# One stationary operand of 96 columns in the last tile's transform back over y

## The chip, the cores and the metric

The kernel runs on 1 core of one Trainium2 chip. The metric is the device time of one execution in microseconds (us), as the median of several runs; beside it stands one profiled execution, from which all views of the trace come.

## The reference, cut to what matters

The input x has 64 samples of 96 channels of 56 by 56 pixels. Layer 0 normalizes it, computes for each of the 6144 (sample, channel) images a 7 by 7 filter of its own by a small network, convolves every image with its filter (zero padding 3), and adds the result to x. Layer 1 treats the result as tokens of 96 channels: a Fourier mixer over the 3136 tokens of a sample, then a feed-forward network in 8-bit floats.

```
weight = a.reshape(b * c, 1, KS, KS)
out = jax.lax.conv_general_dilated(xin, weight, window_strides=(1, 1),
    padding=[(pad, pad), (pad, pad)], feature_group_count=b * c, ...)
x = x + _L0_conv_ref(_gn(x), ...)
t = _to_tokens(x)
t = t + _L1_attn_ref(_ln_t(t), ...)
t = t + _L1_ffn_ref(_ln_t(t), ...)
```

## The kernel before, in words

The program has two phases, one after the other: `conv_layer` (line 699) writes x1 to device memory, and `fourier_layer` (line 1313) reads it. They use the same on-chip memory in turn, so the second phase's pools open when the first one's close.

*Convolution phase.* The 6144 images are cut into tiles of at most 126 (`ROWS`, line 149): 48 tiles of 126 and a last one, tile 48, of 96. The convolution is done as a product in the frequency domain: transforms of the image over y and x as small matmuls, a product with the filter's spectrum, and transforms back over x and over y. Between the steps over x and over y the data goes through device memory (`turn_x`, `turn_y`) to bring another index onto the partitions.

*The transform back over y.* An image's 56 columns are handled in 7 chunks of 8, and the chunks in groups (0,1), (2,3), (4,5), (6). For each chunk `load_x` (line 1104) loads V from `turn_y`: 128 partitions (two halves of 64) by 4 sets of the tile's images. There are 3 buffers for V. `back_y` (line 1108) then takes, for each of the 4 sets and each half, V's images as the stationary operand (64 rows by the images as columns) and the constant `inv_y` as the moving one (64 rows by 56 columns). The result has the images on partitions, in two PSUM banks for a group, one for each half. The images are cut into pieces of 64: a tile of 126 has operands of 64 and 62 columns, the last tile of 64 and 32. After a group, `keep_even` (line 1140, ScalarE) copies the even half to a buffer e (there is one), and `apart` (line 1130, VectorE) makes sum and difference into a buffer o (there are two); `store` (line 1151) writes o to x1, two transfers for a chunk. In the profile these tiles are called V, s (the PSUM banks), e, o and x.

*Order of the work.* Each phase puts its steps, with a cost and a due time each, into a `Plan` (line 292); `emit` (line 344) plays them against a model of the engines and calls them in the order that comes out. All engine calls go through a helper that pins this order on each engine, which is why the profile gives line 505 for every instruction. The step of `back_y` has the planned cost 0.48 us for each chunk (line 1241), whatever the tile. All loads and stores of the phase are issued by SyncE (SP), in order; a transfer that has to wait for a buffer holds up what is queued behind it.

*Around the end of the phase.* Tile 48 is the last one through every step, so its `back_y` is the last work of the phase on TensorE. The Fourier phase then loads its constants (`dft`, `inv`) from ScalarE's queue and its first tokens (`t` from `x`) from SP's queue.

Of the kernel before, what the change touches and what calls it, by code (L numbers as in the profile page):

```python
# [698 lines left out]
def conv_layer(tc, nc, x, x1, b0, attn_bias, weights, a, f, con):  # L699
# [6 lines left out]
    with ExitStack() as ctx:  # L706
# [8 lines left out]
        def bank(name, tag="ps"):  # L715
            return psp.tile([128, BANK], F32, tag=tag, bufs=BUFS1[tag], name=name)
# [117 lines left out]
        def images(i):  # L834
            return min(ROWS, n_rows - i * ROWS)

        def tile_(i, T, at, e0):

            r0 = i * ROWS
            n = images(i)  # L840
# [267 lines left out]
            def back_y(cs):  # L1108


                for half in range(2):
                    v["s4", cs[0], half] = bank(f"s4_{i}_{cs[0]}_{half}")
                for at_, c in enumerate(cs):
                    for e in range(4):
                        other = 6 - e if e < 3 else 7
                        lo = CHUNK // 2 * at_
                        for half in range(2):
                            for a in range(0, n, 64):
                                z = min(a + 64, n)
                                both = v["s4", cs[0], half][a:z, lo : lo + CHUNK // 2].rearrange(  # L1120
                                    "p (x y) -> p x y", x=8
                                )
                                rows_ = slice(64 * half, 64 * half + 64)
                                nc.tensor.matmul(
                                    both[:, e : other + 1 : other - e],
                                    v["V", c][rows_, e * ROWS + a : e * ROWS + z], inv_y[rows_],
                                    start=True, stop=True,
                                )
# [82 lines left out]
            def convolve(T):  # L1211
# [21 lines left out]
                for cs in ((0, 1), (2, 3), (4, 5), (6,)):  # L1233
                    c0, k = cs[0], len(cs)
                    R = T + 2 * PERIOD1 + 14 + e0 * PERIOD1 + K * cs[-1]
                    s4 = [nm("ps", "s4", c0, half) for half in range(2)]
                    o, even = nm("o", c0), nm("e", c0)
                    for c in cs:
                        add(R - 6 - K * (cs[-1] - c) - 31.9, "SP", 0.5, lambda c=c: load_x(c),
                            r=[("dy", i, q) for q in range(4)], w=[nm("V", c)], lag=3.0)  # L1240
                    pe(R + 19.3, 0.48 * k, lambda cs=cs: back_y(cs), r=[nm("V", c) for c in cs],
                       w=[*s4, even, o], kind="halves")
                    add(R - 36.3, "ACT", 0.2 + 0.22 * k, lambda cs=cs: keep_even(cs), r=[s4[0], sm],
                        w=[even])
                    add(R + 103.7, "DVE", 0.12 + 0.54 * k, lambda cs=cs: apart(cs), r=[s4[1], even],
                        w=[o])
                    for c in cs:
                        add(R + 11.8 + c - c0, "SP", 0.8, lambda c=c: store(c), r=[o], lag=3.0)
# [764 lines left out]
```

## Time and profile before

| | us |
|---|---|
| median of 3 runs | 6463.43 (6441.33 to 6465.24) |
| profiled execution, its own time | 6475.86 |
| span in the profile | 6474.1 |
| TensorE matmul (PE) busy | 6132.8 (95%) |
| TensorE weight load (PEld) busy | 4108.4 |
| VectorE (DVE) busy | 4812.8 |
| ScalarE (ACT) busy | 4352.8 |
| GpSimd (POOL) busy | 1891.7 |
| mean granted TensorE clock | 0.975 of full speed |

How to read it: busy times are of one profiled execution. Matmuls overlap in the array, so a group's busy time and the mean duration of one instruction don't tell at what rate they follow each other; for that one looks at start times. A kernel's fp32 matmul appears as two passes, each with a weight load, in the records. In 40 equal slices of the span, PE is busy nine tenths or more in all but four slices: the first, the last, and two from 2266 to 2590 us where the convolution phase ends, with 8 and 7 tenths; the granted clock is down to 5 tenths in the second of these.

```profile
PE   8999999999999987999999999999999999999997
...
PEclk9999999999999995999999999999999999999998
```

### The profile page before, as it was taken

The page shows a single profiled execution, that of the slowest core. Times are in us where ns is not written, and L with a number is a line of the kernel's source. Part 1 is how long each engine was busy: PE and PEld are TensorE (multiplying, and loading weights), DVE is VectorE, ACT ScalarE, POOL GpSimd, SP SyncE. Part 2 cuts the span into 40 slices and gives each one's busy share as a digit, 9 for nine tenths or more (in the row PEclk, how much of TensorE's full clock was granted, in tenths as well). Part 3 has the DMA queues.
Part 4 walks back from the last instruction along what each step waited for, and adds up shares of the span by engine and source line. Part 5 has one row for each costly group of instructions (what it writes and reads, how often), then busy time and mean ns, then how long its engine had stood idle before and what let it go on. Part 6 is the DMA issues. An engine that isn't in the chain of part 4 may idle for free.

```text
span 6474.1 us, 219839 instructions
## 1 busy us (share of the span) xinstructions
PE 6132.8 (95%) x88899; PEld 4108.4 (63%) x88899; DVE 4812.8 (74%) x10984; ACT 4352.8 (67%) x10262; POOL 1891.7 (29%) x1816
## 2 busy tenths in 40 slices
PE   8999999999999987999999999999999999999997
PEld 3444444444444445877777777777777777777774
DVE  4555555555555642788888888988998899899988
ACT  3444444444444441788888888888888888888887
POOL 0222222122222220133333333333333333333334
PEclk9999999999999995999999999999999999999998
DMA  4677777777777876677777778777787787877775
GB/s 130 177 211 220 214 221 220 214 223 219 214 220 214 221 203 161 192 206 225 221 223 230 225 218 231 227 224 229 227 227 220 223 228 225 232 226 230 225 211 163
DMA packets 1325193, 1387.43 MB, mean 214 GB/s; under 512 B 738395, under 2 KB 1190558, under 8 KB 1317145
## 3 DMA queue, kind: packets, MB, share of 16 engines
q1 hardware_dynamic: 1322408, 1363.79, 74.5%
q8 instruction: 701, 11.49, 0.8%
q10 hardware_dynamic: 1769, 9.57, 0.5%
q14 instruction: 315, 2.58, 0.1%
HBM read 744.77 MB, written 628.13 MB: 212 GB/s over the span
## 4 chain that ended last, share of the span: by engine, by line
PE 28%; DMA 14%; ACT 9%; DVE 7%; issue 4%; SPq 1%; POOL 1%; POOLq 0%; ACTq 0%; DVEq 0%
PE l_psum L505 27%; DMA mv<-norms 3%; DMA Y<-turned 3%; ACT h L505 3%; DMA norms<-mr 2%; ACT t L505 2%; DMA nb<-copies 2%; DMA U<-turned 2%; SPq L505 1%; DVE h L505 1%; ACT y L505 1%; PE s L505 1%; DVE x L505 1%; DVE mv L505 1%; DVE g L505 1%
## 5 line engine op out<-in xcount | busy, mean ns | idle before, releaser
L505 PE MATMUL pm<-w0g,xT 128*126 128x512 f32 (+3 forms) x2450 | 1129.3, 602 | 3.0 <-ACT xT L505 3.0
L505 POOL TENSOR_TENSOR t<-t,t 128x504 f32<-128x504 f32 (+1 forms) x392 | 489.9, 1255 | 1954.2 <-DVE t L505 1953.9
L505 POOL TENSOR_TENSOR t<-t,y 96x448 f32<-96x448 f32 x448 | 607.4, 1356 | 1380.5 <-DVE y L505 1032.9
L505 PE MATMUL l_psum<-w1c,t 96*64 96x193 f32 (+1 forms) x7168 | 858.9, 348 | 37.9 <-DMA t<-x 16.7
L505 PEld LDWEIGHTS pm<-w0g,xT 128*126 128x126 f32 (+3 forms) x2450 | 434.0, 188 | 518.1 <-issue 511.3
L505 POOL TENSOR_TENSOR nb<-t,nb 96x448 f32<-96x448 f32 x448 | 532.9, 1194 | 708.1 <-DMA nb<-copies 610.9
L505 ACT COPY B<-s 120x504 f32<-120x504 f32 (+1 forms) x392 | 207.6, 580 | 775.3 <-PE s L505 719.3
L505 ACT COPY t<-l_psum 128x384 f32<-128x384 f32 (+1 forms) x1408 | 644.8, 493 | 57.1 <-PE l_psum L505 56.3
L505 ACT CAST h<-l_psum 128x448 f16<-128x448 f32 x1344 | 667.5, 566 | 14.6 <-PE l_psum L505 14.3
L505 DVE SCALAR_TENSOR_TENSOR g<-l_psum,st,nb 120x192 f32<-120x192 f32 x1792 | 646.3, 409 | 11.5
L505 PE MATMUL l_psum<-dft,Y 112*64 112x112 f32 (+1 forms) x11264 | 629.7, 263 | 4.5 <-DMA Y<-turned 1.8
L505 PEld LDWEIGHTS l_psum<-dft,Y 112*64 112x64 f32 (+1 forms) x11264 | 550.4, 138 | 125.5 <-issue 75.1
L505 DVE TENSOR_TENSOR t<-s,W 128x504 f32<-128x504 f32 (+1 forms) x784 | 481.3, 671 | 182.5 <-PE s L505 182.5
L505 PEld LDWEIGHTS l_psum<-w1c,sq 96*64 96x64 f32 (+1 forms) x7168 | 575.0, 138 | 46.5 <-ACT sq L505 1.9
L505 PE MATMUL l_psum<-inv,U 120*64 120x112 f32 (+1 forms) x7168 | 422.0, 265 | 61.3 <-DMA U<-turned 22.7
L505 PEld LDWEIGHTS l_psum<-inv,U 120*56 120x56 f32 (+1 forms) x7168 | 346.9, 134 | 171.3 <-ACT mr L505 39.9
L505 PEld LDWEIGHTS l_psum<-w1c,t 96*56 96x56 f32 (+1 forms) x7168 | 399.6, 138 | 85.0 <-issue 44.6
L505 PE MATMUL l_psum<-w1c,sq 96*64 96x1 f32 (+1 forms) x7168 | 451.5, 183 | 1.3 <-ACT sq L505 1.3
L505 PE MATMUL l_psum<-g,dft 56*64 56x192 f32 x7168 | 432.4, 340 | 14.3 <-DVE g L505 5.5
L505 DVE CAST h<-h 128x1344 fp8e5<-128x1344 f16 x448 | 413.9, 924 | 14.0 <-ACT h L505 10.4
L505 DVE COPY A<-s 128x504 f32<-128x504 f32 (+1 forms) x343 | 219.6, 674 | 267.2 <-PE s L505 240.3
L505 POOL TENSOR_SCALAR w<-w 128x448 f32<-128x448 f32 (+3 forms) x512 | 273.7, 536 | 464.5 <-DVE w L505 460.4
(127 smaller groups left out, 12513.3 us busy)
## 6 DMA issues: line engine op xcount, KB each, us to landing
turned<-t SPq DMA_DIRECT2D x640, 384.0 KB
nb<-copies SPq DMA_DIRECT2D x448, 336.0 KB
Y<-turned SPq DMA_DIRECT2D x192, 672.0 KB
Y<-turn_x SPq DMA_DIRECT2D x768, 110.2 KB
turn_y<-B SPq DMA_DIRECT2D x768, 110.2 KB
V<-turn_y SPq DMA_DIRECT2D x336, 252.0 KB
U<-turned SPq DMA_DIRECT2D x896, 90.0 KB
t<-x SPq DMA_DIRECT2D x448, 168.0 KB
```

What stands on the lines that cost most here:

```text
L505: ins = issue(*args, **kw)
```

## The change

In `back_y` the width into which a tile's images are cut becomes 64 only for tiles of more than 96 images; a smaller tile is taken in one piece. Only the last tile is smaller: its 96 images become one stationary operand of 96 columns instead of two of 64 and 32, and its 112 matmuls become 56. Nothing else is edited; the planned costs are the same.

```diff
             def back_y(cs):
 
 
+                width = 64 if n > 96 else n
                 for half in range(2):
                     v["s4", cs[0], half] = bank(f"s4_{i}_{cs[0]}_{half}")
                 for at_, c in enumerate(cs):
...
                         for half in range(2):
-                            for a in range(0, n, 64):
-                                z = min(a + 64, n)
+                            for a in range(0, n, width):
+                                z = min(a + width, n)
                                 both = v["s4", cs[0], half][a:z, lo : lo + CHUNK // 2].rearrange(
```

## The prediction

> **What bounds the kernel now.** I read the page first (PE busy 95% of the span), and then asked which stage the 56 removed matmuls stand in. All instructions carry one line number, so I went by tile names: the groups of the convolution phase, kept apart by shape, show what the change touches (count | busy us, mean ns of one | idle before).
>
> ```profile
> L505 PE MATMUL s<-inv_y,V 64*64 64x56 f32 x5488 | 256.8, 228 | 133.1 <-ACT B L505 67.4 <-DMA V<-turn_y 37.5 <-ACT W L505 25.9
> ...
> L505 PE MATMUL s<-inv_y,V 64*62 64x56 f32 x5376 | 226.7, 225 | 0.0
> ...
> L505 PE MATMUL s<-inv_y,V 64*32 64x56 f32 x112 | 21.9, 297 | 0.0
> ```
>
> Each fp32 matmul is two passes in the records. The 48 tiles of 126 images use 64 and 62 columns; only the last tile uses 64 and 32: 112 matmuls, 224 passes. By mean duration they look harmless (297 ns against 228), but matmuls overlap, so durations say little. The timeline of the PE does say it; tile 47 first (32 passes are one chunk):
>
> ```profile
> 2461.58 2.08 PE L505 MATMUL s<-inv_y,V 64*64 64x56 f32 x64 [4.26 <-DMA V<-turn_y]
> 2463.95 1.11 PE L505 MATMUL s<-inv_y,V 64*64 64x56 f32 x32 [0.29 <-DMA V<-turn_y]
> 2468.98 2.11 PE L505 MATMUL s<-inv_y,V 64*64 64x56 f32 x64 [3.92 <-DMA V<-turn_y]
> 2472.12 1.11 PE L505 MATMUL s<-inv_y,V 64*64 64x56 f32 x32 [1.03 <-DMA V<-turn_y]
> 2474.48 1.23 PE L505 MATMUL s<-inv_y,V 64*64 64x56 f32 x32 [1.25 <-DMA V<-turn_y]
> ```
>
> Then the chain that ended last, where tile 48 does the same amount of passes:
>
> ```profile
> 2474.00 2.97 DMA V<-turn_y
> 2477.11 38.92 PE s L505 x220
> ...
> 2516.11 0.45 ACT e L505
> ...
> 2517.88 5.13 DMA x<-o
> ...
> 2525.93 9.00 DMA t<-x
> ```
>
> 224 passes take 7.6 us of PE in tile 47 and 38.9 us in tile 48, and those 38.9 us are one unbroken piece of the chain. The windows (PE, PEld, DVE, ACT, POOL busy, then clock, DMA share, GB/s) show that nothing covers them, and that the clock is the same, half, in both tiles:
>
> ```profile
> 2461.50:2476.50 15.00, 7.64 (x224) 6.86 (x224) 3.81 (x8) 2.35 (x4) 0.00 (x0) 0.50 0.85 221
> 2477.10:2516.10 39.00, 38.99 (x222) 25.32 (x222) 3.44 (x6) 1.89 (x3) 0.00 (x0) 0.50 0.26 68
> 2516.10:2533.40 17.30, 0.63 (x4) 0.31 (x5) 0.73 (x4) 0.44 (x1) 0.83 (x8) 0.50 0.81 196
> 2533.40:2617.00 83.60, 75.72 (x830) 61.82 (x832) 31.85 (x99) 33.23 (x100) 2.24 (x4) 0.57 0.59 168
> 2617.00:6474.00 3857.00, 3710.79 (x66120) 2860.32 (x66115) 3385.76 (x8222) 3256.93 (x8414) 1398.14 (x1404) 0.99 0.77 221
> ```
>
> The Fourier layer starts only after this tail: its first load (t<-x) is issued once the last convolution store (x<-o) has landed, and it reuses the memory. So the tail is a serial seam of the program: whatever it loses, the span loses.
>
> **The change, part by part.**
>
> *Removed: 112 matmuls alternating between 64 and 32 columns.* In tile 48 one pair (64, then 32 columns) takes 38.92 / 56 = 0.695 us, so 0.35 us per matmul; in tile 47 a matmul takes 2.08 / 32 = 0.065 us. The surplus, 38.9 - 7.6 = 31.3 us, comes with the alternation of widths, because moving operand, clock and neighbours are the same. Here a rule of the skill speaks against the change: "TensorEngine Tiling (Array Packing)", Theoretical Speedup, says that operands of at most 64 by 64 let four tiles of the array work at once, so that one operand of 96 columns, which needs the whole width, leaves two. By that rule alone the old form would run in rounds of four passes as in tile 47 (56 rounds x 0.11 = 6.2 us), and the change would cost some 3 us. The row says 38.9. The same page (Key Properties) has the reason: changing the tiling mode, and not just the tile, drains the engine. 64 and 32 columns are two modes, 64 and 62 one. I take the row.
>
> *Added: 56 matmuls (112 passes) of 96 columns, all of one mode,* on two tiles of the array (rows 0-63 and 64-127), which write to different banks. No row shows this shape. From tile 47: (2.08 - 0.31 of the last pass) / 16 = 0.111 us for a round of four passes with 64 columns to load, 1.73 ns per column. From this:
> - if the round follows the weight load: 96 x 1.73 = 0.166 us, 56 rounds = 9.3 us;
> - if it follows the moving operand (56 columns as before): 0.111 us, 6.2 us;
> - if the two halves do not overlap: 112 x 0.166 = 18.6 us; if a drain remained at each matmul, 56 x 0.35 = 19.6 us.
>
> I take 9.3 us, 1.33 us per chunk instead of 5.56, as tile 47 shows that passes on different parts of the array overlap when the width stays. A negative cost beyond this is excluded: it would need less than no time for 112 passes.
>
> *Moved: nothing.* The order and the waits of ACT, DVE, POOL and SP are the same in the changed kernel, and those of PE outside these matmuls (the planner's costs are not edited). Tiles of 126 images keep width 64.
>
> *What is late next.* With PE fast, the tail becomes a loop of loads and stores in SP's queue. V has 3 buffers, so the load of chunk 3 waits for chunk 0, and SP issues in order: V3, V4, four stores of chunks 0 and 1, V5, V6, then stores. I replay it with durations of before (V load 2.97, e 0.63 and 0.44, o 1.15 and 0.68, four stores 1.74, two 0.78):
> - chunks 0, 1, 2: 2477.1 to 2481.2 (their V were issued at 2474.00 and 2476.03, before the tail; unchanged);
> - V3 issued at 2478.6 (before: 2482.84), lands 2481.6; chunk 3 to 2483.0, chunk 4 to 2484.4;
> - chunks 0 and 1 read out: e, o from 2480.0 to 2481.95, stores issued until 2483.7; behind them V5 and V6, landing 2486.7 and 2487.2;
> - chunk 5 to 2488.1, chunk 6 to 2489.4; the last o until about 2491.2; the last store issued by 2492.6.
>
> Before, the last store was issued by 2518.3 (2517.53 + 0.78): 25.7 us saved. I charge 0.7 us because the stores of chunks 4 and 5 now run just ahead of the last one and share its landing (5.13 us before): 25 us. So of 29.6 us that PE saves, 4 to 5 turn into waits for V. If V loads take 4.99 us, as tile 47 shows once under traffic, at both places: 21. With PE at 18.6 to 19.6 us the loads hide mostly behind it: about 20. With PE at 6.2: 27.
>
> *After the seam* the same Fourier work follows, 25 us earlier; it is bound by PE and by its own waits, and nothing in it is tied to a point in time, so I let the gain arrive at the end whole.
>
> The profiled execution took 6475.9 us (span 6474.1 plus 1.8 around it); less 25 it would be 6450.9. It lies 12.4 us above the median of the runs, 6463.4, from which I forecast: 6463.4 - 25 = 6438 us, -0.39%.
>
> **The rivals.**
> - *The two halves run one after the other, or the drain stays with each matmul.* PE 18.6 to 19.6 us, gain 20: 6443 us. For it: no row shows two row halves with 96 columns. Against it: tile 47's rounds of four. Chance 0.13.
> - *The granted clock comes back earlier as well.* From 2456 on PE runs at half clock, until 2617. The window 2533.40:2617.00 has 75.7 us of busy PE at 0.57; were the clock back 26 us sooner there, about half of that, 13 us, would be gained on top: 6425 us. For it: the pattern of busy and idle time ahead of it changes. Against it: this stretch stays at half clock through 80 us of one repeating pattern, so its own small gaps seem to hold it there, and these move along unchanged. Run-to-run spread (6441 to 6465) works in the same direction or against it. Chance 0.23.
> - *Slower: the stretch at half clock grows.* A shorter tail with PE busy only some 9 of 15 us gives the clock less reason to return. Work after 2617 has PE busy 96% of the time, so each us more at half clock costs about half a us. It loses the 25 us only from 50 us more on, and reaches +0.5% from 115 us on: then about 6496 us. Against it: the last line of the windows has 0.99 for all 3857 us. Chance 0.02.
> - *The change does nothing to the time,* because the tail is covered. Against it: PE's 38.9 us stand in the chain, POOL waits for them in one piece, and DMA share is 0.26 there. Chance 0.02.
>
> The main case has 0.60.
>
> **How the numbers follow.** About 0.5% (32 us) is what a measurement of this kernel can tell from no change; the forecast of 25 us lies below it, so "within 0.5%" is likeliest. The main case (20 to 27 us, and a spread of some 12 us either way between runs) crosses 32 us one time in five: 0.12; the clock case mostly does: 0.20; the first rival rarely: 0.01. Faster 0.33, slower 0.01, same 0.66. The range, from the clock case (6425, less some spread) to the gain of 20 with a slow draw: 6417 to 6456.
>
> **What would show it.** Right: the 224 passes of tile 48 become 112, the piece of the chain at 2477 breaks up into pieces of 2 to 4 us with V<-turn_y between them; the last x<-o about 25 us earlier; the Fourier windows the same length. Wrong: 112 passes still in one piece of about 19 us (first rival), or the gain at the seam is there but the stretch at half clock has another length (second and third). The forecast is wrong also if the first t<-x is held by something other than the last store, and so does not move with it.

## The result and the profile after

The median went from 6452.74 us (19 runs) to 6425.87 us (19 runs); the ratio of the two is 0.9957, with a 95% interval of 0.9946 to 0.9968. That is 0.43% faster, 20.6 to 34.8 us. The forecast was 25 us, or 0.39%. Measured again later on another chip, the changed kernel gave 0.9958 (0.9946 to 0.9971) of the kernel before.

The profiled execution took 6423.8 us, with a span of 6422.0: 52 us less than the profile of before. Half of that lies outside the stretch in which the changed matmuls stand, as will be seen; so I read that stretch itself. First the group that replaced the columns of 64 and 32 (count | busy us, mean ns | idle before):

```profile
L505 PE MATMUL s<-inv_y,V 64*96 64x56 f32 x112 | 9.9, 365 | 4.6 <-DMA V<-turn_y 4.6
```

One of these passes lasts longer on average than one of the old groups (365 ns against 297 and 228), and yet PE's busy time for the tile fell from 38.9 to 9.9 us: again the durations of overlapping matmuls say nothing, their spacing does. PE's timeline of tile 48 and the first Fourier matmul:

```profile
2471.14 4.26 PE L505 MATMUL s<-inv_y,V 64*96 64x56 f32 x48 [2.29 <-DMA V<-turn_y]
2476.68 2.81 PE L505 MATMUL s<-inv_y,V 64*96 64x56 f32 x32 [1.27 <-DMA V<-turn_y]
2480.52 2.81 PE L505 MATMUL s<-inv_y,V 64*96 64x56 f32 x32 [1.03 <-DMA V<-turn_y]
2502.01 0.90 PE L505 MATMUL l_psum<-w1c,t 96*64 96x193 f32 x4 [18.68 <-DMA t<-x]
```

The one unbroken piece has become three (chunks 0 to 2, then 3 and 4, then 5 and 6) with a wait for a V load ahead of each. In the chain that ended last the place of the 38.9 us is taken by short pieces of every kind:

```profile
2471.14 2.79 PE s L505 x30
...
2474.01 0.64 ACT e L505
...
2474.67 1.16 DVE o L505 x2
...
2477.68 2.80 DMA V<-turn_y
...
2480.52 2.86 PE s L505 x32
...
2486.26 5.16 DMA x<-o
...
2494.31 9.08 DMA t<-x
```

The windows (columns as in the prediction: the tile, the gap up to the first Fourier matmul, the stretch at half clock after it):

```profile
2471.10:2483.40 12.30, 9.89 (x112) 9.39 (x112) 2.90 (x6) 1.89 (x3) 0.00 (x0) 0.50 0.68 180
2483.40:2502.00 18.60, 0.00 (x0) 0.02 (x1) 1.27 (x6) 0.44 (x1) 0.82 (x8) 0.50 0.89 215
2502.00:2573.00 71.00, 64.65 (x618) 51.72 (x620) 21.47 (x76) 24.09 (x77) 0.00 (x0) 0.50 0.60 174
```

I call *seam* the time from tile 48's first matmul in `back_y` to the first Fourier matmul. Before, that matmul stands here:

```profile
2533.42 0.90 PE L505 MATMUL l_psum<-w1c,t 96*64 96x193 f32 x4 [16.70 <-DMA t<-x]
```

So the seam was 2533.42 - 2477.11 = 56.3 us and is 2502.01 - 2471.14 = 30.9 us: 25.4 us shorter. The other 26.7 us between the two spans lie outside it: 6.0 us ahead of the tile (2477.11 against 2471.14), and 20.7 us in the Fourier phase (6474.1 - 2533.4 against 6422.0 - 2502.0). The last experiment asks whether the latter belong to the change.

### The profile page after: what moved, and what is told of

Its sections match the earlier page's. It is cut to its first block, busy times and chain, and to the rows that moved or that the text cites. A ratio compares the mean times of both kernels' runs of the same rounds, so it can differ in the third digit from the quotient of the medians.

```text
span 6422.0 us, 219615 instructions
## 1 busy us (share of the span) xinstructions
PE 6101.9 (95%) x88787; PEld 4087.7 (64%) x88787; DVE 4811.4 (75%) x10984; ACT 4352.4 (68%) x10262; POOL 1889.5 (29%) x1816
## 4 chain that ended last, share of the span: by engine, by line
PE 32%; DMA 11%; ACT 9%; DVE 6%; issue 4%; SPq 1%; POOL 1%; POOLq 0%; ACTq 0%; DVEq 0%
PE l_psum L505 30%; DMA Y<-turned 3%; ACT h L505 3%; DMA mv<-norms 2%; ACT t L505 2%; DMA U<-turned 1%; SPq L505 1%; ACT y L505 1%; DVE h L505 1%; DMA nb<-copies 1%; DMA norms<-mr 1%; DVE g L505 1%; DVE CD L505 1%; ACT p L505 1%; DVE t L505 1%
## 5 line engine op out<-in xcount | busy, mean ns | idle before, releaser
L505 DVE SCALAR_TENSOR_TENSOR g<-l_psum,st,nb 120x192 f32<-120x192 f32 x1792 | 646.6, 409 | 11.5
L505 PEld LDWEIGHTS l_psum<-w1c,t 96*64 96x64 f32 (+1 forms) x7168 | 398.5, 138 | 84.1 <-issue 46.6
L505 PEld LDWEIGHTS l_psum<-inv,U 120*64 120x64 f32 (+1 forms) x7168 | 347.8, 134 | 161.5 <-ACT mr L505 40.1
L505 DVE CAST h<-h 128x1344 fp8e5<-128x1344 f16 x448 | 415.3, 927 | 13.9 <-ACT h L505 10.2
```

What stands on the lines that cost most here:

```text
L505: ins = issue(*args, **kw)
```

## The experiments

Two theories at the outset. **A**: what costs is the change of the operand's width between one matmul and the next, about 0.35 us each at half clock; the tail is a serial seam, and what it saves arrives at the end. **B**: what costs is the narrow operand, or the number of matmuls. After the first runs the question was what bounds the seam now, and whether the clock has a part in it.

**The same matmuls in another order.** Two kernels keep the last tile's 112 matmuls of 64 and 32 columns and only sort them: inside a chunk (14 changes of width), or inside each set (56).

```diff
+                cuts = [(a, min(a + 64, n)) for a in range(0, n, 64)]
+                todo = [(e, half, a, z) for e in range(4) for half in range(2) for a, z in cuts]
+                if n <= 96:
+                    todo.sort(key=lambda t: t[2])
...
+                    for e, half, a, z in todo:
```

This is the order inside the chunk. The other kernel differs in the key of the sort, which keeps the four sets (`e`) apart:

```diff
+                    todo.sort(key=lambda t: (t[0], t[2]))
```

> The last tile keeps its 112 matmuls of 64 and 32 columns; within a chunk all of 64 columns come first, then all of 32: 14 changes of width in the tile instead of 112. Theory A (each change of width costs about 0.35 us at half clock, the shape nothing): 112 matmuls take about 8 rounds of two at 0.11 us for each width and two changes, some 2.2 us a chunk, 15 us in all instead of 38.9; the end of the tile is then set by the V loads, and from the tile's first matmul to the last store takes 16 to 19 us instead of 40.8; time as the changed kernel, about 0.4% below the kernel before. Theory B (operands of 32 columns are slow in themselves, or 112 matmuls are too many): no change, 38 to 40 us and the time of the kernel before.

> Same 112 matmuls of 64 and 32 columns in the last tile; within each of the 4 sets the two of 64 columns come first, then the two of 32: 56 changes of width, half of those before. Theory A: half of 38.9 us, 19 to 21 us of PE for the tile; from the first matmul to the last store about 22 us instead of 40.8; time about 0.3% below the kernel before. Theory B: no change against the kernel before.

PE's windows of the tile, for inv_y's instructions alone (PE and PEld busy, clock, DMA share, GB/s), first the one sorted in the chunk:

```profile
2471.30:2486.70 15.40, 11.54 (x224) 9.88 (x224) 0.72 0.53 140
```

and the one sorted in the set:

```profile
2470.50:2490.90 20.40, 20.32 (x224) 13.33 (x224) 0.50 0.41 108
```

In the kernel before, the tile is one piece of PE's timeline (second profile, in which no record is missing):

```profile
2474.07 39.62 PE L505 MATMUL s<-inv_y,V 64*64 64x56 f32 x224 [2.62 <-DMA V<-turn_y]
```

Both came out as A says, and B's "no change" is gone: the same 224 passes take 39.6 us of PE with 112 changes of width, 20.3 with 56, and 11.5 with 14. From 112 to 56 that is 0.345 us for each change avoided. (With 14 changes part of the tile ran at full clock, 0.72 on average, so that step isn't a pure price.) Sorting also makes the two halves alternate more often, but that isn't what saves the time: tile 47 and the kernel of the next experiment keep the old order of the halves, and neither pays. The seams were 33.4 and 37.4 us, the ratios to the kernel before 0.9968 (0.9954 to 0.9981) and 0.9974 (0.9962 to 0.9986). From the seams one would work out -22.9 us (-0.35%) and -19.0 us (-0.29%): both lie inside the intervals.

**More and narrower matmuls, one width.**

```diff
+                cuts = [(a, min(a + (64 if n > 96 else 32), n)) for a in range(0, n, 64 if n > 96 else 32)]
+                todo = [(e, half, a, z) for e in range(4) for half in range(2) for a, z in cuts]
...
+                    for e, half, a, z in todo:
```

> The last tile is cut into three operands of 32 columns: 168 matmuls (336 passes) instead of 112, and no change of width within it. Theory A: they overlap in rounds of up to six, 56 rounds at about 0.1 us, 6 to 12 us of PE for the tile; the tail is as in the changed kernel (about 15 us from first matmul to last store); time about 0.4% below the kernel before. Theory B (the number of matmuls or the narrow operand costs): 168 x 0.35 = 58 us of PE, the time 0.3% above the kernel before.

PE's timeline of tile 48 in this kernel:

```profile
2468.82 1.83 PE L505 MATMUL s<-inv_y,V 64*32 64x56 f32 x96 [1.55 <-DMA V<-turn_y]
2471.40 1.09 PE L505 MATMUL s<-inv_y,V 64*32 64x56 f32 x48 [0.74 <-ACT e L505]
2474.51 1.83 PE L505 MATMUL s<-inv_y,V 64*32 64x56 f32 x96 [2.02 <-DMA V<-turn_y]
2480.00 1.91 PE L505 MATMUL s<-inv_y,V 64*32 64x56 f32 x96 [3.66 <-DMA V<-turn_y]
```

336 passes take 6.7 us, less than the 9.9 of the changed kernel with 112. This is the clearest word against B: half as many matmuls again as before, all as narrow as the narrowest, and the cost is gone. It also shows that the seam has another bound by now: with 3.2 us less on PE it is 31.9 us, no shorter than the changed kernel's 30.9 (ratio 0.9962, 0.9946 to 0.9977).

**The same fault where PE is busy and at full clock.** As the changed kernel, and tiles 20 to 29 are cut into 64, 32 and 30 columns.

```diff
+                cuts = [(0, 64), (64, 96), (96, n)] if 20 <= i < 30 else [(0, 96)] if n == 96 else [(0, 64), (64, n)]
...
```

> As the changed kernel, and ten tiles in the middle of the convolution phase (20 to 29, 126 images each) are cut into 64, 32 and 30 columns, so that the width changes twice in each of their 560 triples: 1120 changes at full clock. Theory A with the cost paid away from the seam too (PE is busy 95% of this stage): at 0.2 to 0.35 us a change about 220 to 390 us more than the changed kernel, 6650 to 6820 us. Theory A with slack (PE's busy time there is waiting that would be absorbed): under 100 us more. Theory B (an operand of 32 columns costs 0.35 us each, 1120 of them): the same size, so this run only measures the price outside the seam.

The median is 6794.4 us, a ratio of 1.0503 (1.0479 to 1.0526) to the kernel before. Against 0.9957 of that kernel's 6467.2 us, that is 355 us for 1120 changes, 0.32 us each. The trace has nearly all of it in place: by start times, from the first matmul of tile 20 in `back_y` to the last one of tile 29 this kernel takes 816.7 us (1242.6 to 2059.3), the changed one 472.3 (1243.8 to 1716.1), 344 us less. So the price is paid in full; there is no slack in this stage to take it. The trace adds something that none of the theories had (the ten tiles in this kernel; columns as in the prediction's windows):

```profile
1243.00:2060.00 817.00, 798.62 (x5537) 449.81 (x5534) 274.30 (x522) 216.07 (x348) 99.45 (x80) 0.80 0.46 126
```

In the changed kernel the clock is 1.00 in the first two thirds of the same tiles, and on to 2300 us:

```profile
1243.00:1560.00 317.00, 301.79 (x2931) 151.75 (x2928) 185.19 (x351) 137.72 (x226) 67.33 (x54) 1.00 0.79 221
1560.00:2300.00 740.00, 704.37 (x6931) 359.18 (x6927) 433.44 (x820) 333.84 (x546) 153.55 (x124) 1.00 0.78 216
```

The records call PE busy for 98% of the stage with the mixed widths, and still the granted clock stood at half for 39% of it. By start times, a triple of 64, 32 and 30 columns takes 0.466 us at full clock and 0.713 us at half. In the changed kernel the two matmuls in its place (64 and 62 columns, four passes) take 0.058 us at full clock. So a change of width costs about 0.2 us there at full clock, (0.466 - 0.058) / 2. The rest of the 0.32 I put down to the slower clock, under which the triples and their neighbours ran; no run separates the two.

**What bounds the seam now.** The largest constant of the Fourier phase is loaded behind 21 loads of tokens instead of ahead of the first.

```diff
-        inv2 = const("inv2", [4 * K1, HALF, RI])
+        inv2 = cp.tile([4 * K1, HALF, RI], F32, name="inv2")
+        loads = []
...
                     nc.sync.dma_start(tokens[c], x1b[:, CHUNK * c : CHUNK * (c + 1)])
+                    loads.append(c)
+                    if len(loads) == 21:
+                        nc.sync.dma_start(inv2, con["inv2"])
```

> The changed kernel, and the Fourier phase's largest constant (inv2, 1470 KB) is loaded on SP's queue after 21 loads of tokens instead of ahead of the first. Theory (after the change the seam is bound by transfers: 5.2 us for the last store to land, then 10.2 us from the first token load to the first Fourier matmul, both shared with 2.4 MB of constants): the 10.2 us shrink to 4 to 7, and the rest of the seam is as in the changed kernel (20.6 us from the tile's first matmul to the first token load); 4 to 6 us faster than the changed kernel, about -0.08%. Rival (the token loads wait for something else, the seam stays 30.9 us): no change. The runs can hardly tell either in the time; the seam's parts in the trace do.

A second run of it stands on one chip with the changed kernel:

> The late load of inv2 beside the changed kernel. If its shorter seam (22.9 us against 30.9) arrives at the end: 8 us, 0.12%, below the changed kernel, which is hardly more than these runs tell apart; if the load is only moved to where it is waited for, the same time.

The chain of the second run around the seam's end, and its first Fourier matmul:

```profile
2491.78 4.74 DMA x<-o
...
2497.22 2.37 DMA t<-x
...
2499.59 0.90 PE L505 MATMUL l_psum<-w1c,t 96*64 96x193 f32 x4 [10.82 <-DMA t<-x]
```

From the issue of the first token load (2496.87) to that matmul it takes 2.7 us, where the changed kernel takes 10.2 (2491.76 to 2502.01). The seam is 22.9 us in the first profile and 23.1 in the second, 7.8 less than in the changed kernel and thus more than the 4 to 6 expected. The constant isn't waited for later either: its first reader stands 118.1 and 117.3 us behind the first Fourier matmul, against 118.0 and 119.5 in the two profiles of the changed kernel. The times: 0.9937 (0.9914 to 0.9959) and 0.9934 (0.9911 to 0.9957) of the kernel before, where the changed kernel had 0.9958 on the same chip. The late load is thus faster than the kernel before beyond doubt. By its seam it is 8 us faster than the changed kernel; the runs alone can't settle that, the two intervals overlap.

**The clock.** The second rival of the prediction asked whether the clock would come back earlier. Here 80 matmuls that nothing reads fill PE's gap in the seam, alone and together with the late load.

```diff
         plan.emit()
+        w2a, spare = weights["w2a"], bank("spare")
+        for _ in range(80):
+            nc.tensor.matmul(spare[:C, :C], w2a, w2a, start=True, stop=True)
```

> The changed kernel, and 80 matmuls that nothing reads (96 columns, 96 moving, on constants) follow the last one of the convolution phase, to keep PE busy in the gap. It asks about the clock: in both kernels PE is at half clock for some 71 us after the first Fourier matmul. If the clock is held down by the idle time of the seam: it is at full speed when the Fourier phase starts, and that stretch is some 15 to 30 us shorter, time 0.2 to 0.4% below the changed kernel. If the stretch's own gaps hold it down (the reason given with the prediction): the clock falls back within some 10 us of the start, the stretch is as long as before, and the time is that of the changed kernel, or up to 8 us more where the added matmuls run past the gap.

> The late load and the added matmuls together. If both theories hold, the gains add up: 0.3 to 0.5% below the changed kernel. If the stretch's own gaps hold the clock down: as the late load alone, less what the added matmuls run past the shorter gap (up to 13 us more).

The gap and the 70 us after it, in the kernel with the added matmuls alone, and PE's timeline at the gap:

```profile
2485.80:2503.90 18.10, 14.75 (x164) 14.60 (x162) 1.42 (x6) 0.45 (x1) 0.83 (x8) 0.95 0.87 212
...
2503.90:2574.00 70.10, 63.10 (x603) 50.44 (x605) 20.82 (x73) 23.59 (x76) 0.00 (x0) 0.51 0.61 176
...
2485.81 14.72 PE L505 MATMUL spare<-w2a 128*96 128x96 f32 x160
2503.88 0.54 PE L505 MATMUL l_psum<-w1c,t 96*64 96x193 f32 x4 [3.35 <-DMA t<-x]
```

The clock was brought back within the gap (0.95), and by the clock's records it fell to half again 0.9 us after the first Fourier matmul. The stretch at half clock ended 72.6 us after that matmul, where the changed kernel has 70.7 and the kernel before 72.0. This looks as if the stretch's own gaps held the clock down, but it can't tell the two theories apart: the added matmuls ended 3.35 us too early, so PE stood idle right ahead of the stretch.

With the late load as well there is no such gap, and the clock held for 14.8 us:

```profile
2499.90:2514.60 14.70, 11.36 (x189) 9.59 (x191) 6.74 (x24) 6.30 (x20) 0.00 (x0) 1.00 1.01 250
```

It then fell within the stretch and stayed at half until 66.0 us after the first Fourier matmul. So the gap of the seam isn't needed to bring the clock down; what in the stretch brings it down was not traced. While the clock was full it helped: the third group g<-dft started 13.1 us after the first Fourier matmul, against 19.0 with the late load alone, and 4.0 of these 5.9 us were left from the fifth group on. They were lost again ahead of the stretch, as the added matmuls ran past the tokens' arrival: the seam is 27.4 us, 4.3 to 4.5 longer than with the late load alone. The times are 0.9941 (0.9918 to 0.9964) and 0.9946 (0.9926 to 0.9966), not to be told from the changed kernel. Nothing was gained by the added matmuls; what a clock that stays up through the stretch would bring is open.

**What the rest of the 52 us was.** Both kernels, profiled once more.

> The changed kernel once more, for a second profiled execution and to stand beside the late load on one chip. Theory: the seam (first matmul of the last tile to first Fourier matmul) is 30.9 us again within 0.5; the length of the Fourier phase after it, which was 3920.0 us in the changed kernel's first profile and 3940.7 in that of before, differs from the first by some 10 to 30 us although the kernel is the same. Rival (the change shortens the Fourier phase too): 3920 again, within 3 us.

> The kernel before once more, for a second profile. Theory: seam 56.3 us again within 0.5, and a Fourier phase that differs from the 3940.7 us of the first profile by up to 30 us either way. Rival: 3940.7 again within 3 us, so that the 20.7 us between the first two profiles are an effect of the change.

| | seam, us | Fourier phase, us |
|---|---|---|
| before, first and second profile | 56.3, 56.1 | 3940.7, 3955.2 |
| changed, first and second profile | 30.9, 30.7 | 3920.0, 3962.8 |

The seam repeats within 0.3 us. The Fourier phase of one and the same kernel differs by 43 us between two executions, more than the 20.7 us in question, and in the second pair it is the changed kernel that takes longer. So those 20.7 us are no evidence of an effect of the change; what spreads this phase so was not traced further. The start of tile 48 moves too, by some 3 us within one kernel (2477.1 and 2474.1 before, 2471.1 and 2473.8 after). A difference of spans between two single profiles would have told a gain twice as large as the seam's.

## Why the prediction was right

*The surplus comes with the change of width.* Right, and now shown: 112, 56, 14 and no changes give 39.6, 20.3, 11.5 and 6.7 us (the last with 168 matmuls). The page "TensorEngine Tiling (Array Packing)" of the Trainium skill says under Key Properties that a change of mode drains the engine. The price of a change fits this: 0.345 us at half clock and about 0.2 at full. That it is a drain, no trace shows. The rule that more tiles can work at once (the page has the four tiles of 64 by 64 under The Solution, and a factor of up to two for each dimension of at most 64 under Theoretical Speedup) also fits once the widths are equal, 6.7 us for thirds against 9.9 for one operand of 96, but it was never the bound.

*96 columns in rounds of 0.166 us.* Right: 32 passes take 2.81 us, less 0.365 for the last one, over 15 intervals is 0.163 us for a round of two. The estimate took the weight load as the bound; the one by the moving operand (0.111) and the serial one (0.33) are excluded. Between the first two the prediction gave no reason for its choice; overlap in tile 47 speaks for both. PE took 9.9 us instead of 9.3, mostly because each of the three pieces ends with the whole length of a last pass.

*What is late next.* Right: V loads, in the places that the replay had them. SP's queue in the changed kernel:

```profile
2472.88 1.92 SPq L505 DMA_DIRECT2D V<-turn_y  x2
2475.84 1.74 SPq L505 DMA_DIRECT2D x<-o  x4
2477.68 0.98 SPq L505 DMA_DIRECT2D V<-turn_y  x2
2480.13 6.56 SPq L505 DMA_DIRECT2D x<-o  x10
```

V3 was issued 1.7 us after the tile's first matmul (replay 1.5), and the last store was issued by 15.5 us after it (replay 15.5). Of the 29.7 us that PE saved, 25.4 reached the first Fourier matmul.

*The 0.7 us charged for the landing.* Not seen: the last store in the chain landed in 5.16 us (5.13 before), and the token load in the chain in 9.08 (9.00).

*The gain arrives whole.* The seam's 25.4 us are 0.39% of the time, and the measured ratio (two measurements, 0.43% and 0.42%) contains it in its interval. No run shows a further effect behind the seam; one of a few us, either way, would be lost in these intervals.

*The level.* The forecast of 6438 us started from a median of three runs of before; with 19 runs that median is 6452.7 instead of 6463.4. That is why the time is lower than the forecast although the gain fits.

*The rivals.* Halves one after the other, or a drain at each matmul: excluded by the rounds of 0.163 us. A clock that comes back earlier: the stretch at half clock after the first Fourier matmul is 70.7 and 72.3 us in the two profiles of the changed kernel, 72.0 and 71.7 in those of before. A longer stretch: excluded by the same numbers. A covered tail: excluded by the 25.4 us that reached the first Fourier matmul.

*The clock, where the prediction misread it.* It has PE at half clock from 2456 to 2617 us. By the clock's records that stretch ran from 2445.0 to 2605.5; the window 2533.40:2617.00 with its 0.57 holds 72 us at half and then 11.5 at full. The reason that it gave for the stretch, small gaps of its own, remains open, as the experiment with the added matmuls showed. Neither touches the forecast, since the change left the stretch as it was.

## What to carry to other kernels

In these runs matmuls on parts of the array overlapped only while all of them divided it in the same way (64 with 62 columns, 32 with 32, 96 with 96; not 64 with 32). When a remainder makes two widths alternate, sort by width, or choose one width for all, even if that means wider operands or more matmuls. Look at the last, odd tile of a phase by itself, since a tile with 2% of its step's matmuls can hold a seam that nothing covers. Judge matmuls by the spacing of their starts, and a gain at a seam by the seam's length, which here repeats within 0.3 us where whole executions differ by tens.

## What I had not expected of the hardware

A stretch in which matmuls of different widths alternate is busy by the records (98%) and is granted half the clock for 39% of the time (0.80 on average, against 1.00 for the same tiles with equal widths). That the drained array counts as idle for the clock would explain it, but this is argued, not shown. And some 70 us of Fourier work stay at half clock although PE is busy for 90% of them by the records (63.10 of 70.10); entered at full clock and without a gap, this work kept it for 14.8 us and then lost it.
